# An attention block in fp32: how the second group's tokens are turned, and three places in VectorE's order

## The chip, the cores and the metric

The kernel runs on one core of a Trainium2 chip. A core has TensorE (matrix products, results into PSUM), VectorE, ScalarE and GpSimd (elementwise work), SyncE (which here only issues DMAs) and 16 DMA engines between the chip's memory (DRAM) and SBUF. Each engine works through its own list of instructions in order; a semaphore makes an instruction wait for another engine or for a DMA's landing. The metric is the device time of one execution in microseconds (us), lower is better. In the profile PE is TensorE, PEld its weight loads, DVE VectorE, ACT ScalarE, POOL GpSimd and SP SyncE; a `q` after a name (SPq) marks the engine's sequencer, which issues DMAs.

## The reference

The input `x` is 64 batches of 128 tokens with 512 features, all fp32. The reference normalises each token, takes 16 heads of queries (64 wide) and one head of keys and values that all heads share, puts a learned null key and value in front, adds an attention bias for each head, masks later tokens and masked tokens, and takes the softmax. The heads' results go through an output matrix, are normalised once more and are added to `x`:

```
xn = layernorm(x, g_in)
q = (xn @ Wq).reshape(b, n, H, DH).transpose(0, 2, 1, 3) * scale
k, v = split(xn @ Wkv);  null key and value in front
sim = einsum('bhid,bjd->bhij', q, k) + bias;  causal and token mask
out = einsum('bhij,bjd->bhid', softmax(sim), v) @ Wo
x = x + layernorm(out, g_out)
```

## The kernel before

The batches are worked on in groups of four (`GB = 4`; group g holds batches 4g to 4g+3) and in pairs. For each group the normalised tokens must stand with features on partitions (`xT[g]`), since TensorE multiplies along partitions. There are two ways to get there. `norm_T` (line 306 on) has TensorE transpose a batch's four 128x128 blocks against an identity into PSUM, and ScalarE copies them out in three pieces. `tokens_T` (line 321 on) has VectorE transpose 32x32 blocks in SBUF into a tile `xb`; when four such tiles are there, `tokens_out` stores `xb` to a DRAM buffer `xd` and `tokens_in` reads it back in four loads, in the order wanted. Before the change groups 0 and 1 go by `norm_T`, groups 2 to 15 by the other way. The two ways need different tiles from DRAM: for `norm_T` a tile is one batch (128 rows of `x[m]`, line 120), for `tokens_T` it is 32 tokens of each of the group's four batches (line 122). `xs[m]` is that tile for place m; place 4 lives in `wM`.

Everything stands in the order in which the program writes it (a manual schedule): the list at the file's end (from line 1559 on) for groups 0 and 1, then `body_first`, then `turn(d)` and `body(d)` for the pairs, `turn_end` and `body_end` for the last two pairs, and `body_last`. No planner moves anything.

In the first part stand, in this order on their engines: statistics of the tiles (`norm_stats`: three small VectorE operations and a power on GpSimd, line 281), the keys' and values' product (`kv_pair`, `kv_pair_out`: VectorE writes `vT` at line 380, ScalarE `kT` at line 390), the causal mask on the bias (`causal`, GpSimd, line 212), the subtraction of the null bias (`null_shift`, VectorE, line 229), mask and bias together (`bias_add`, GpSimd, line 683), scores on TensorE (line 718) and their addition to the bias on VectorE (lines 733 and 735), the exponentials on ScalarE (line 749). The queries of group 0 are full products (`q_mm`, line 450, copied out at line 459), those of later groups seven products of halves (`product`, line 515), in which product 7 adds into a PSUM tile after ScalarE has kept what was there (`keep`, line 527, tile `ku`). For these, VectorE makes sums of weights (line 483) and GpSimd sums of tokens (`token_sum`, line 497).

DMAs are nearly all issued by SyncE, in order, and each carries one of eight semaphores in turn: a DMA is issued only when the DMA eight places ahead of it has landed. In `body_end` the output products add into one PSUM tile (`py_s`) in turn; VectorE copies an intermediate result out (`out_keep` of `yu2`, line 948, tile `kyu`) and TensorE's next product into that tile waits for the copy.

## Time and profile before

| | us |
|---|---|
| median of 3 runs | 1023.34 (1023.27 to 1023.65) |
| profiled execution | 1022.89 |
| its span, first to last instruction | 1021.0 |
| TensorE busy in the span | 1013.0 (99%) |
| VectorE busy | 845.7 (83%) |
| GpSimd busy | 768.6 (75%) |
| ScalarE busy | 673.2 (66%) |

The profiled execution is 1.9 us longer than its span, which counts from the first to the last instruction. A row of the timeline gives start, duration, engine, line, operation, tiles written and read, and how many instructions it merges; in brackets stands how long the engine was idle before it and what ended that. TensorE's clock was granted at 0.998 of full speed.

### The profile page before, as it was taken

The page shows a single profiled execution, that of the slowest core. Times are in us where ns is not written, and L with a number is a line of the kernel's source. Part 1 is how long each engine was busy: PE and PEld are TensorE (multiplying, and loading weights), DVE is VectorE, ACT ScalarE, POOL GpSimd, SP SyncE. Part 2 cuts the span into 40 slices and gives each one's busy share as a digit, 9 for nine tenths or more (in the row PEclk, how much of TensorE's full clock was granted, in tenths as well). Part 3 has the DMA queues.
Part 4 walks back from the last instruction along what each step waited for, and adds up shares of the span by engine and source line. Part 5 has one row for each costly group of instructions (what it writes and reads, how often), then busy time and mean ns, then how long its engine had stood idle before and what let it go on. Part 6 is the DMA issues. An engine that isn't in the chain of part 4 may idle for free.

```text
span 1021.0 us, 31459 instructions
## 1 busy us (share of the span) xinstructions
PE 1013.0 (99%) x12333; PEld 901.6 (88%) x12333; DVE 845.7 (83%) x1958; ACT 673.2 (66%) x2753; POOL 768.6 (75%) x633
## 2 busy tenths in 40 slices
PE   9999999999999999999999999999999999999997
PEld 9888888888888888888888888888988888888886
DVE  6777888888888888888888888888898888977787
ACT  5766677656677665686656776566775657865583
POOL 4997768677686877859678696776868768686686
PEclk9999999999999999999999999999999999999999
DMA  7415243151431415225152340514314152140221
GB/s 218 139 30 150 67 125 111 34 154 63 145 97 69 123 56 152 87 75 140 35 152 85 109 123 29 164 63 138 103 49 134 64 153 89 70 113 24 69 85 62
DMA packets 73835, 100.86 MB, mean 99 GB/s; under 512 B 32212, under 2 KB 36056, under 8 KB 71896
## 3 DMA queue, kind: packets, MB, share of 16 engines
q1 hardware_dynamic: 73392, 98.47, 32.3%
q8 instruction: 96, 1.57, 0.6%
q14 instruction: 51, 0.42, 0.1%
q10 hardware_dynamic: 296, 0.40, 0.1%
HBM read 63.19 MB, written 33.55 MB: 95 GB/s over the span
## 4 chain that ended last, share of the span: by engine, by line
PE 97%; POOL 1%; DVE 1%; issue 0%; ACT 0%; POOLq 0%; DVEq 0%
PE pyX L936 20%; PE pa L515 16%; PE pyY L936 10%; PE pc L515 10%; PE po L849 8%; PE pkv L363 6%; PE pyw L936 5%; PE pl L581 4%; PE pm L647 4%; PE ps L718 3%; PE pq L450 3%; PE sc_X L718 2%; PE sc_Y L718 2%; PE sc_a L718 1%; PE py_s L936 1%; PE busy L1556 1%
## 5 line engine op out<-in xcount | busy, mean ns | idle before, releaser
L749 ACT ACTIVATE s<-s,nmax 128x65 f32<-128x65 f32 (+1 forms) x1024 | 372.1, 369 | 61.7 <-DVE nmax L740 61.7
L771 POOL TENSOR_TENSOR s<-s,rinv 128x512 f32<-128x512 f32 (+1 forms) x132 | 190.6, 1446 | 132.7 <-DVE rinv L767 132.7
L683 POOL TENSOR_TENSOR s<-biasp,mneg 128x1552 f32<-128x1552 f32 (+1 forms) x65 | 206.3, 3177 | 51.0 <-DVE s L733 27.0
L749 ACT ACTIVATION_READ_ACCUMULATOR s<-s,nmax 128x1 f32 x1024 | 197.0, 192 | 0.0
L787 DVE STREAM_TRANSPOSE sb<-s 128x1536 f32<-128x1536 f32 (+1 forms) x68 | 113.6, 1674 | 11.3 <-POOL s L771 11.3
L740 DVE TENSOR_REDUCE nmax<-s 128x8 f32<-128x1032 f32 (+1 forms) x128 | 121.7, 951 | 0.1
L964 ACT COPY y<-pyX 128x256 f32<-128x256 f32 x29 | 10.8, 372 | 167.5 <-PE pyX L936 161.2
L936 PE MATMUL pyX<-wT,oT 128*128 128x256 f32 x464 | 109.8, 380 | 0.0
L936 PE MATMUL pyX<-wo,oT 128*128 128x256 f32 x464 | 109.7, 380 | 0.0
L936 PEld LDWEIGHTS pyX<-wo,oT 128*128 128x128 f32 x464 | 86.2, 191 | 10.4
L936 PEld LDWEIGHTS pyX<-wT,oT 128*128 128x128 f32 x464 | 84.2, 191 | 9.1
L916 POOL TENSOR_TENSOR oT<-oT 128x512 f32<-128x512 f32 x64 | 80.5, 1277 | 3.9 <-PE pyw L936 1.6
L527 ACT COPY ku<-pa 128x256 f32<-128x256 f32 x118 | 43.4, 367 | 59.7 <-issue 30.8
L849 PE MATMUL po<-sb,vr 32*64 32x128 f32 (+1 forms) x3904 | 81.8, 308 | 0.0
L849 PEld LDWEIGHTS po<-sb,vr 32*64 32x64 f32 x3904 | 71.4, 131 | 8.3 <-issue 5.9
L536 DVE TENSOR_TENSOR qT<-pc,ku 128x256 f32<-128x256 f32 x118 | 48.1, 408 | 32.2 <-PE pc L515 19.9
L868 ACT ACTIVATE oT<-po,nv 128x512 f32<-128x512 f32 (+1 forms) x127 | 73.5, 655 | 0.5 <-PE po L849 0.4
L515 PE MATMUL pa<-xS,wq 128*128 128x256 f32 x264 | 67.8, 380 | 0.0
L597 DVE TENSOR_TENSOR qT<-pl,kp 128x128 f32<-128x128 f32 x112 | 32.0, 286 | 42.8 <-PE pl L581 41.9
L281 POOL TENSOR_TENSOR rstd<-rstd,nhalf 128x1 f32<-128x1 f32 x64 | 35.2, 558 | 42.2 <-DVE rstd L280 39.3
L363 PE MATMUL pkv<-xT,wkv 128*128 128x256 f32 x256 | 63.4, 391 | 0.0
L515 PE MATMUL pa<-xT,wq 128*128 128x256 f32 x236 | 60.6, 380 | 0.0
(207 smaller groups left out, 2591.9 us busy)
## 6 DMA issues: line engine op xcount, KB each, us to landing
res<-in_x_dram SPq DMA_DIRECT2D x64, 256.0 KB
out_dram<-y SPq DMA_DIRECT2D x63, 256.0 KB
x<-in_x_dram SPq DMA_DIRECT2D x62, 256.0 KB
xd<-xb SPq DMA_DIRECT2D x14, 1024.0 KB
xT<-xd SPq DMA_DIRECT2D x56, 256.0 KB
vr<-vd SPq DMA_DIRECT2D x64, 128.0 KB
kT<-kT SPq DMA_DIRECT2D x32, 64.0 KB
vd<-vb SPq DMA_DIRECT2D x32, 64.0 KB
```

The source lines that it names most:

```text
L363: nc.tensor.matmul(pkv, wkv[:, kc, :], xT[g][:, t : t + 2, kc, :], start=(kc == 0), stop=(kc == KC - 1),)
L515: nc.tensor.matmul(prod[tag], w[:, kc, f * P : (f + 1) * P], t[:, :, kc, :], start=(start and kc == 0), stop=(kc == HK - 1), skip_group_ch ...
L683: nc.gpsimd.tensor_tensor(S[b][:, :, keys], biasp[:, :, keys], mneg[:, t, keys] .unsqueeze(1) .broadcast_to([P, R8, keys.stop - keys.start ...
L718: nc.tensor.matmul(home[r][u * DH : (u + 1) * DH, f, :], qT[g, f, t // 2][rows, t % 2, hf, u], kT[rows, 0 : nk // Q, t, :], start=True, st ...
L740: nc.vector.tensor_reduce(nmax[b][:, hf], S[b][:, :, WITH_NULL[hf]], AX.X, ALU.max, negate=True)
L749: nc.scalar.activation(row, row, AF.Exp, bias=nmax[b][:, hf, k : k + 1], accum_out=rsum[b][:, hf, k : k + 1],)
L771: nc.gpsimd.tensor_tensor(sv, sv, rinvs[b, hf][:, lo:hi].unsqueeze(2).broadcast_to([P, hi - lo, sv.shape[2]]), ALU.mult,)
L787: nc.vector.transpose(sbs[b][:, :, lo:hi].rearrange("p j e q -> p e j q"), S[b][:, lo:hi, 1 : ROW - 1].rearrange("p e (j k) -> p e j k", k=Q),
L849: nc.tensor.matmul(po[s][rows, to : to + n], vr[g][quad, t, PLACE[j], :], sb[quad, slots, r * NF : (r + 1) * NF, :], start=(turn == 0), st ...
L868: nc.scalar.activation(to, src, AF.Identity, bias=nv2)
L916: eng.tensor_tensor(o, a, b, op)
L936: nc.tensor.matmul(prod[key], h[:, c, :], w[:, c, :], start=(start and c == 0), stop=(c == HC - 1), skip_group_check=not start,)
```

## The change

Group 1 goes by `tokens_T`, `tokens_out` and `tokens_in` instead of `norm_T`, so its four tiles are loaded by line 122. Three query products (columns 0, 1 and 2 for the group's second half of batches) now stand ahead of the second batch's scores, where there were two, and the first two of them are done in two halves of tokens each. `token_sum(1, 1)` and `(1, 2)` are written later, which leaves GpSimd's order as it was. In `body_end` a maximum over scores (`scores_max(b, 1)`) moves behind the copy `kyu`; in `body_last` the last statistics of one tile move ahead of the sum for the other.

```diff
-        if g < 2:
+        if g == 0:
             queue.dma_start(out=xs[m], in_=x[m])
         else:
             nc.sync.dma_start(
                 out=xs[m], in_=x[g * GB : (g + 1) * GB, t * Q : (t + 1) * Q, :]
...
-    def q_batches(cs):
+    def q_batches(cs, h=0):
...
         scale(b, 0)
-        scores_max(b, 1)
         out_product(p, 6, ps_s, "s", start=False)
         out_keep("s", "yu2", "yu2")
+        scores_max(b, 1)
...
         nc.vector.bn_stats(st[0][:, 1], ys[p][:, hi_e])
+        mv, rstd = last_stats(p, st[0])
         out_product(p, 7, ps_q, "c", start=False)
         out_part(p + 1, 1, "c", "yp5")
-        mv, rstd = last_stats(p, st[0])
...
-    norm_T(4)
+    tokens_T(4)
...
-    norm_T(5)
+    tokens_T(5)
     mask_neg(0)
     q_batches((6,))
-    norm_T(6)
+    tokens_T(6)
+    tokens_T(7)
+    tokens_out(1)
+    tokens_in(1)
     null_shift(0)
     bias_add(0, (slice(0, UK.start), slice(UK.start, ROW)))
     q_half(7, 0)
-    norm_T(7)
...
+    q_batches((0,), 1)
     exps(0, 0, 0, 4)
-    q_half(0, 1)
+    q_batches((1,), 1)
     exps(0, 0, 4)
-    q_half(1, 1)
+    q_half(2, 1)
```

On SyncE, in the first 20 us: `x_202`, `x_204`, `x_206` and `wM` are the tiles of places 5, 6, 7 and 4, `nkv` the null key and value, `biasp` the bias.

```order
 L174 DMA wkv<-in_L_cond_Wkv_dram 128x4x128
 L175 DMA wq<-in_L_cond_Wq_dram 128x4x512
-L120 DMA wM<-in_x_dram 128x512
-L120 DMA x_202<-in_x_dram 128x512
-L120 DMA x_204<-in_x_dram 128x512
-L120 DMA x_206<-in_x_dram 128x512
+L122 DMA wM<-in_x_dram 128x1x512
+L122 DMA x_202<-in_x_dram 128x1x512
+L122 DMA x_204<-in_x_dram 128x1x512
+L122 DMA x_206<-in_x_dram 128x1x512
 L180 DMA nkv<-in_cond_dram 128x1
 L198 DMA biasp<-in_fside_16xSxS_dram 64x4x64
```

The four loads keep their places and take the other form; further down SyncE's list, behind `vr` and ahead of `nv`, come the store to `xd` and the four loads of `xT`.

On VectorE, around the two subtractions of the null bias (line 229):

```order
 L289 TENSOR_SCALAR nmr_383<-mv_326,rstd_328 128x1
 L289 TENSOR_SCALAR nmr_385<-mv_340,rstd_342 128x1
+L326 STREAM_TRANSPOSE xb_399<-wM 128x4x4x32
 L225 COPY nbp<-nbh 64x8
 L229 TENSOR_TENSOR biasp<-biasp,nbp 64x8x192
+L326 STREAM_TRANSPOSE xb_399<-x_202 128x4x4x32
+L326 STREAM_TRANSPOSE xb_399<-x_204 128x4x4x32
+L326 STREAM_TRANSPOSE xb_399<-x_206 128x4x4x32
 L225 COPY nbp<-nbh 64x8
 L229 TENSOR_TENSOR biasp<-biasp,nbp 64x8x192
```

One transpose comes ahead of the first subtraction, three ahead of the second.

On VectorE in `body_end`, here for the pair before the last; first before the change, where `nmax` is the result of the maximum:

```order
L1142 TENSOR_SCALAR lrs_12982<-lmv_12980 128x1
L966 TENSOR_TENSOR y_13007<-pyw_2_13002,kyp_12989 128x256
L767 RECIPROCAL rinv_0_13011<-rsum_12991 128x8
L740 TENSOR_REDUCE nmax_12955<-s_12763 128x8
L948 COPY kyu_13020<-py_1_s 128x256
L767 RECIPROCAL rinv_1_13026<-rsum_12947 128x4
```

and after it:

```order
L1142 TENSOR_SCALAR lrs_12969<-lmv_12967 128x1
L966 TENSOR_TENSOR y_12994<-pyw_2_12989,kyp_12976 128x256
L767 RECIPROCAL rinv_0_12998<-rsum_12978 128x8
L948 COPY kyu_13006<-py_1_s 128x256
L740 TENSOR_REDUCE nmax_12942<-s_12750 128x8
L767 RECIPROCAL rinv_1_13013<-rsum_12934 128x4
```

Copy and maximum have changed places; nothing else in the pair has.

More of the change, by code (lines that the diff above doesn't have):

```diff
@@ L466, in q_half @@
         q_copy(pq, c, h)
-    def q_batches(cs):
-        pqs = [q_room(c, 0) for c in cs]
+    def q_batches(cs, h=0):
+        pqs = [q_room(c, h) for c in cs]
         for t in range(2):
             for pq, c in zip(pqs, cs):
-                q_mm(pq, c, 0, slice(t, t + 1))
+                q_mm(pq, c, h, slice(t, t + 1))
         for pq, c in zip(pqs, cs):
-            q_copy(pq, c, 0)
+            q_copy(pq, c, h)
     def weight_sum(k):
@@ L1631 @@
     bias_add(2)
+    q_batches((0,), 1)
     exps(0, 0, 0, 4)
-    q_half(0, 1)
+    q_batches((1,), 1)
     exps(0, 0, 4)
-    q_half(1, 1)
+    q_half(2, 1)
     rinv(0, 0)
     scale(0, 0)
-    token_sum(1, 1)
-    token_sum(1, 2)
     scores(1, 0, ((ps_y, "X"), (ps_w, "w")))
@@ L1645 @@
     scores_max(1, 1)
+    token_sum(1, 1)
+    token_sum(1, 2)
     exps(0, 1, 0, 4)
-    q_half(2, 1)
     exps(0, 1, 4)
```

## The prediction

> **What bounds the kernel now.** First the table of windows over one long stretch: its bounds and length, then busy time of TensorE, its weight loads, VectorE, ScalarE and GpSimd, clock, DMA share and GB/s.

> ```profile
> 10.00:960.00 950.00, 950.00 (x11464) 847.27 (x11463) 789.37 (x1832) 634.29 (x2590) 718.80 (x581) 1.00 0.34 99
> ```

> From 10 to 960 us TensorE has no idle time (950.00 of 950.00). Work taken from it there is a gain only if nothing else becomes late, and a stall put into the start is never won back: there is no later gap to swallow it. So I looked at who else runs close to the edge before 60 us. Timeline rows of VectorE, GpSimd, ScalarE and of TensorE's weight loads, start and duration first:

> ```profile
> 18.12 0.14 DVE L373 TENSOR_SCALAR nkv<-nkv 64x1 f32<-64x1 f32 x1
> ...
> 20.67 7.35 POOL L212 TENSOR_SCALAR_AFFINE_SELECT biasp<-biasp 64x512 f32<-64x512 f32 x6
> ...
> 23.56 1.75 DVE L229 TENSOR_TENSOR biasp<-biasp,nbp 64x1536 f32<-64x1536 f32 x1 [1.16 <-POOL biasp L212]
> ...
> 28.06 1.75 DVE L229 TENSOR_TENSOR biasp<-biasp,nbp 64x1536 f32<-64x1536 f32 x1 [2.21 <-POOL biasp L212]
> ...
> 29.96 9.73 POOL L683 TENSOR_TENSOR s<-biasp,mneg 128x520 f32<-128x520 f32 x4 [1.93 <-DVE biasp L229]
> ...
> 36.55 0.42 DVE L733 TENSOR_TENSOR s<-sc_w,s 128x256 f32<-128x256 f32 x1 [0.50 <-POOL s L683]
> ...
> 36.55:53.63 17.08, 17.08 (x81) 15.07 (x80) 16.73 (x24) 11.68 (x58) 17.00 (x11) 1.00 0.40 126
> ...
> 52.35 0.49 DVE L380 TENSOR_SCALAR vT<-pkv,nkv 64x256 f32<-64x256 f32 x1
> ...
> 52.92 0.76 ACT L390 ACTIVATE kT<-pkv,nkv 64x128 f32<-64x128 f32 x3 [2.27 <-DVE vT L380]
> ...
> 54.59 0.37 ACT L527 COPY ku<-pa 128x256 f32<-128x256 f32 x1 [0.20 <-PE pa L515]
> ...
> 55.04 0.84 PEld L515 LDWEIGHTS pa<-xS,wq 128*128 128x128 f32 x4
> ```

> Read from top to bottom this is one chain beside TensorE. GpSimd applies the causal mask (20.67 to 28.02), VectorE subtracts the null bias as soon as that ends (28.06), GpSimd adds mask and bias as soon as that ends (29.96), VectorE waits for the sums (36.55, 0.50 idle) and then works almost without a break until 53.63 (16.73 of 17.08). ScalarE waits 2.27 for its `vT`, writes `kT`, normalises a tile and copies `ku`; ScalarE could have copied `ku` 0.20 earlier, and TensorE loads the weights of product 7, which needs that copy, 0.08 after it ends (54.96 to 55.04). So the chain lies only 0.20 behind TensorE at 55 us: whatever delays line 373 at 18.12 or the mask at 20.67 by d delays TensorE there by d - 0.20.

> **The change part by part.** *Transposes taken from TensorE.*

> ```profile
> 22.36 0.60 PE L313 MATMUL pxT<-wR,wM 128*128 128x128 f32 x4
> 22.80 1.95 PE L450 MATMUL pq<-xT,wq 128*128 128x128 f32 x16
> 24.58 0.60 PE L313 MATMUL pxT<-wR,x 128*128 128x128 f32 x4
> ...
> 27.24 1.89 PE L450 MATMUL pq<-xT,wq 128*128 128x256 f32 x8
> 28.97 0.60 PE L313 MATMUL pxT<-wR,x 128*128 128x128 f32 x4
> ```

> One batch's four transposes hold TensorE for 0.44 (22.36 to 22.80), so four batches 1.76, and twelve ScalarE copies go with them. But the chain above doesn't use this: of the 1.76 only 0.20 could reach product 7. The two products cut into token halves take 1.78 instead of 1.73 each (22.80 to 24.58; 27.24 to 28.97): 0.1, inside that. Moving one more product ahead of the second scores adds nothing and moves ScalarE's copies little: nothing.

> *Transposes given to VectorE*: four operations like this one.

> ```profile
> 54.42 0.71 DVE L326 STREAM_TRANSPOSE xb<-x 128x512 f32<-128x512 f32 x1 [0.79 <-ACT x L302]
> ```

> The first (0.71) fits into the 1.16 idle before 23.56, the other three (2.13) into the 2.21 before 28.06. Nothing; without that cover 2.84.

> *The loads.* Batches 4 to 7 are now read as 4 batches x 32 tokens (line 122) instead of 128 rows of one batch (line 120). The trace has both. DMA share and GB/s are the last two figures of these windows; the first is in the stretch where line-120 and weight loads run, the others where only the two line-122 loads issued at 54.44 are under way:

> ```profile
> 11.50:12.50 1.00, 1.00 (x11) 1.00 (x11) 0.67 (x2) 0.37 (x1) 0.30 (x1) 1.00 1.07 397
> ...
> 57.50:58.50 1.00, 1.00 (x6) 0.90 (x5) 0.91 (x2) 0.42 (x2) 1.00 (x2) 1.00 0.26 102
> 60.50:61.50 1.00, 1.00 (x55) 0.91 (x57) 0.67 (x3) 0.00 (x0) 0.92 (x2) 1.00 0.27 100
> ...
> 54.44 1.14 SPq L122 DMA_DIRECT2D x<-in_x_dram  x2
> ```

> A line-122 load moves at 100 to 102 GB/s on a quarter of the DMA engines (share 0.26), and two of them issued together still hold only that quarter: they share the same four engines, one after the other. 256 KB takes 2.6 us there, against 0.67 at 397 GB/s. [...]

> ```profile
> SPq L184 <- DMA x<-in_x_dram: 0.7, 1, 0.7
> ...
> 13.78 0.69 DVE L270 BATCH_NORM_STATS2 st<-wM 128x6 f32<-128x512 f32 x1 [0.80 <-DMA wM<-in_x_dram]
> 16.35 0.57 SPq L184 DMA_DIRECT2D nbh<-cond_null_attn_bias_dram  x1
> 19.37 1.07 SPq L200 DMA_DIRECT2D biasp<-in_fside_16xSxS_dram  x2
> ...
> 28.17 1.17 SPq L189 DMA_DIRECT2D nv<-in_cond_dram  x2
> ```

> Batch 4 lands at 13.78 now (VectorE waits for it), so its data start near 13.11; at 2.6 each, batches 4 to 7 land at 15.7, 18.3, 20.9 and 23.5. Batch 7 landed by 16.35 before (that landing lets SyncE issue `nbh`): 7.15 later. Line 373 at 18.12 needs `nkv`, whose small load stands right behind batch 7; I take it 0.3 later, 23.8 (between 0 and the 0.57 of one issue). So VectorE's order, statistics of batches 5 and 6, `nkv`, `vT`, statistics of batch 7, then GpSimd's power and mask, moves by d = 23.8 - 18.12 = 5.7. The bias loads behind `nbh` move by 7.15: the last one, issued by 19.37 + 1.07 = 20.4, would be out by 27.6, and the second half of the mask wants it at 20.67 + 7.35/2 + 5.7 = 30.0: 2.4 us for a small load, just enough, no cost. Product 7 then comes 5.7 - 0.2 = **5.5** later, and with TensorE full up to 960 us so does everything behind it.

> *The round trip through DRAM*: one store and four loads, on SyncE ahead of `nv` and the next tiles.

> ```profile
> 80.03 0.33 SPq L335 DMA_DIRECT2D xd<-xb  x1
> 83.92 1.76 SPq L343 DMA_DIRECT2D xT<-xd  x4
> ...
> 84.30:91.60 7.30, 7.30 (x36) 6.43 (x35) 6.00 (x11) 1.48 (x6) 5.30 (x3) 1.00 0.90 201
> ...
> 40.63 2.28 POOL L497 TENSOR_TENSOR xS<-xT 128x512 f32<-128x512 f32 x1
> ```

> The store takes SyncE's slot of 28.17, 5.7 to 7.15 later: 33.9 to 35.3. The loads go 3.89 after it and their 1.05 MB are in between 5.6 us (at 201 GB/s) and 7.7 us (91.60) later: 43.4 to 46.9. GpSimd's first token sum wants them at 40.63 + 5.7 = 46.3. I take nothing; at the late end 0.6. The next tiles, `wo` and `gob` go out about 6 us later than the rest (3.89 to the loads' issue, 1.76 for it); their users are also later by 5.7, so nothing, with a microsecond of risk.

> *VectorE's order in the last steps.*

> ```profile
> 974.10 1.18 DVE L740 TENSOR_REDUCE nmax<-s 128x8 f32<-128x1032 f32 x1
> 975.19 0.42 DVE L948 COPY kyu<-py_s 128x256 f32<-128x256 f32 x1
> ...
> 975.75 1.97 PE L936 MATMUL py_s<-wo,oT 128*128 128x256 f32 x8 [0.28 <-DVE rinv L767]
> ...
> 994.37 1.97 PE L936 MATMUL py_s<-wo,oT 128*128 128x256 f32 x8 [0.38 <-DVE rinv L767]
> ...
> 999.07 1.91 DVE L787 STREAM_TRANSPOSE sb<-s 128x768 f32<-128x768 f32 x2
> ...
> 1001.04 0.45 PE L849 MATMUL po_s<-sb,vr 32*64 32x256 f32 x4
> ...
> 1012.82 1.27 POOL L1161 TENSOR_TENSOR y<-y,res 128x512 f32<-128x512 f32 x1
> 1014.04 0.55 POOL L1308 TENSOR_TENSOR rstdo<-rstdo,nhalf 128x1 f32<-128x1 f32 x1
> 1015.63 0.43 DVE L1275 BATCH_NORM_STATS2 stl<-pyc 128x6 f32<-128x256 f32 x1
> ```

> With the copy `kyu` ahead of the 1.18 maximum, TensorE's waits of 0.28 and 0.38 go. Next late is VectorE's transpose: it ends at 1000.98 and the last batch's values start at 1001.04, so much of the 0.66 returns there. I take half, **-0.3** (bounds -0.7 and 0). In the very last step the power on GpSimd can't start before the residual ahead of it ends (1014.09), and VectorE's later statistics wait for TensorE: nothing (bounds -0.3 and 0).

> The sum: +5.5 - 0.3 = +5.2. Span 1021.0 + 5.2 = 1026.2; the profiled execution 1022.89 + 5.2 = 1028.1. It ran 0.45 under the median of the runs, 1023.34, so the median after is **1028.5**.

> **The rivals.** *The loads are no later than before* (they spread, or are early enough): then the transposes' gain is cut to 0.2 by `ku`, and with the end's 0.3 the median is 1022.8, no change. This decides if batch 7 lands by 17.8, 0.3 ahead of line 373 at 18.12, so with 1.4 us of delay at most. Against it: the 0.26 share. *The whole gain arrives*: 1.76 + 0.66 = 2.4, 1020.9, faster. It needs the loads early and the chain behind 36.55 shorter; nothing in the change shortens that. *The round trip comes late too*: GpSimd waits at the token sum, or VectorE for the next tiles, 1 to 3 us on top, 1030.5. For it: the token sum's slack ends at -0.6. *TensorE's other stalls*: ScalarE, in order, copies queries behind the mask load, which moves too; if that runs past the chain, up to 1 us more, inside the range.

> **How the numbers follow.** Slow loads holding the chain: 0.79, 1028.5. Its low end: the four engines free 1 us earlier than 13.11 (-1.0), `nkv` and a `vT` (0.3 and, by the row at 52.35, 0.5) not on the way to the mask (-0.8), all 0.7 at the end (-0.4), and the 0.45 between profiled run and median: 1025.8. Round trip late as well: 0.13, up to 1030.5 + 1 for ScalarE + 0.5 = 1032.0. Loads hidden: 0.05. Whole gain: 0.03. The range holds the first two, 0.92 less their tails. A measurement here tells 0.2%, 2 us, from no change: slower 0.92, same 0.05, faster 0.03.

> **What would show it.** Right: `wM` and three tiles landing about 2.6 apart, VectorE idle for x loads between 14 and 24; line 373 near 23.8, the mask near 26.4, line 683 near 35.7; line 326 four times before 34 without moving line 229; product 7's weights near 60.5; no 0.28 and 0.38 in the last steps. Wrong: the mask still near 20.7, or TensorE without idle time before 60 us.

## The result, and the profile after

The changed kernel takes 1036.84 us (median; 1035.96 to 1038.73) against 1023.48 for the kernel before on the same chip: 1.0133 times as long, 95% interval 1.0120 to 1.0145, so 13.4 us slower where 5.2 were forecast; 1036.84 lies above the forecast's upper bound of 1032.0. The profiled execution took 1036.95, its span 1035.2 (before: 1022.89 and 1021.0), TensorE's clock 0.994.

The window that was full before (950.00 of 950.00), in the profile after; columns as in the prediction:

```profile
10.00:960.00 950.00, 940.57 (x11392) 836.74 (x11391) 781.10 (x1812) 625.40 (x2546) 708.34 (x577) 0.99 0.34 100
```

TensorE is idle for 9.4 us of it, and a clock of 0.99 where it was 1.00 says that it also worked more slowly for a while. The timeline after, in the order of the prediction's chain (loads, mask, bias):

```profile
15.56 0.70 DVE L270 BATCH_NORM_STATS2 st<-wM 128x6 f32<-128x512 f32 x1 [2.51 <-DMA wM<-in_x_dram]
...
21.41 0.69 DVE L270 BATCH_NORM_STATS2 st<-x 128x6 f32<-128x512 f32 x1 [1.40 <-DMA x<-in_x_dram]
...
24.40 0.15 DVE L373 TENSOR_SCALAR nkv<-nkv 64x1 f32<-64x1 f32 x1 [1.89 <-DMA nkv<-in_cond_dram]
...
25.11 0.76 ACT L390 ACTIVATE kT<-pkv,nkv 64x128 f32<-64x128 f32 x3 [6.29 <-DVE vT L380]
...
26.18 7.20 PE L450 MATMUL pq<-xT,wq 128*128 128x128 f32 x40 [3.78 <-ACT qT L459]
...
26.97 7.35 POOL L212 TENSOR_SCALAR_AFFINE_SELECT biasp<-biasp 64x512 f32<-64x512 f32 x6
...
31.65 1.90 DVE L326 STREAM_TRANSPOSE xb<-x 128x512 f32<-128x512 f32 x3
...
33.90 1.12 ACT L670 ACTIVATE mneg<-m,neg 128x256 f32<-128x256 uint8 x2 [2.98 <-DMA m<-in_mask_BxS_bk_dram]
...
35.32 0.27 PE L718 MATMUL sc_Y<-kT,qT 64*64 64x64 f32 x1 [1.47 <-ACT qT L459]
...
36.34 1.20 POOL L683 TENSOR_TENSOR s<-biasp,mneg 128x520 f32<-128x520 f32 x1 [2.02 <-DVE biasp L229]
```

The first half is as forecast: tiles one after the other, line 373 at 24.40 (23.8 forecast), the mask at 26.97 (26.4), line 683 at 36.34 (35.7), so the chain is 6.4 late instead of 5.7. New are TensorE's own waits, 3.78 and 1.47, both for ScalarE's copies of queries: ScalarE works in order and stood at `kT` for 6.29 (its releaser `vT` stands behind line 373 on VectorE) and then at the mask tile `m` for 2.98.

From the round trip to product 7:

```profile
36.56 0.37 SPq L335 DMA_DIRECT2D xd<-xb  x1
...
42.60 1.74 SPq L343 DMA_DIRECT2D xT<-xd  x4
...
51.25 1.27 POOL L497 TENSOR_TENSOR xS<-xT 128x512 f32<-128x512 f32 x1 [4.20 <-DMA xT<-xd]
...
53.55 0.69 DVE L270 BATCH_NORM_STATS2 st<-x 128x6 f32<-128x512 f32 x1 [2.77 <-DMA x<-in_x_dram]
...
57.95 0.69 DVE L270 BATCH_NORM_STATS2 st<-x 128x6 f32<-128x512 f32 x1 [3.30 <-DMA x<-in_x_dram]
...
58.97 1.77 DVE L787 STREAM_TRANSPOSE sb<-s 128x1536 f32<-128x1536 f32 x1
...
63.04 0.49 DVE L380 TENSOR_SCALAR vT<-pkv,nkv 64x256 f32<-64x256 f32 x1
...
64.97 0.36 ACT L527 COPY ku<-pa 128x256 f32<-128x256 f32 x1
65.43 2.04 PE L515 MATMUL pa<-xS,wq 128*128 128x256 f32 x4 [4.16 <-ACT ku L527]
```

The store's landing lets the loads go: 36.56 to 42.60, 6.0 us against 3.89 in the later steps of the kernel before. The token sum then waits 4.20, and VectorE waits 2.77 and 3.30 for tiles 8 and 9, which SyncE issues behind these transfers. Tile 9 comes last: behind its statistics stand VectorE's transpose, `vT`, ScalarE's `kT` and `ku` (54.59 before, 64.97 now). Product 7 starts 10.2 late.

The clock, in windows of 3.41 us of the profile after (columns as above; the last three are clock, DMA share, GB/s):

```profile
22.96:26.37 3.41, 0.20 (x1) 0.20 (x2) 1.80 (x6) 1.01 (x4) 0.27 (x2) 1.00 0.26 56
26.37:29.78 3.41, 3.41 (x17) 3.41 (x17) 2.31 (x7) 2.54 (x6) 3.27 (x4) 0.50 0.47 115
...
60.51:63.92 3.41, 0.76 (x4) 0.33 (x2) 3.35 (x8) 0.31 (x2) 3.41 (x3) 1.00 0.20 76
63.92:67.33 3.41, 1.90 (x5) 1.57 (x6) 1.11 (x3) 2.40 (x7) 3.41 (x3) 0.50 0.18 31
67.33:70.75 3.42, 3.42 (x10) 2.70 (x9) 1.55 (x4) 0.74 (x2) 3.42 (x2) 0.50 0.26 86
70.75:74.16 3.41, 3.41 (x54) 2.79 (x55) 2.43 (x3) 1.76 (x4) 3.33 (x3) 1.00 0.17 60
```

After a stretch in which TensorE worked 0.76 of 3.41 us (60.51 to 63.92), its clock is exactly half for two stretches: 5.32 us of work from 65.43 to 70.75 at half speed lose 2.66. The same happened once before, behind the wait of 3.78: 0.20 of 3.41 worked, then a whole stretch at half clock, which loses 1.7. That loss is part of how late TensorE itself comes to product 7 (it is ready for it at 61.27, 6.0 later than product 7 started before), so it isn't to be added to the 10.2. The first maximum over scores behind it comes 12.84 later than before (62.69 to 75.53): 10.2 and 2.6. Up to 147 us about 0.6 more is lost in small steps, the last pair's statistics (line 1275) come at 1029.18 against 1015.63, 13.55 later, and the last 0.65 of the 14.2 by which the span grew lie in the landing of the last stores. For these last two small amounts the traces show no cause.

### The profile page after: what moved, and what is told of

It is laid out like the page before. It is cut to its first block, busy times and chain, and to the rows that moved or that the text cites. A ratio compares the mean times of both kernels' runs of the same rounds, so it can differ in the third digit from the quotient of the medians.

```text
span 1035.2 us, 31459 instructions
## 1 busy us (share of the span) xinstructions
PE 1017.2 (98%) x12333; PEld 902.8 (87%) x12333; DVE 846.6 (82%) x1962; ACT 671.2 (65%) x2741; POOL 766.4 (74%) x633
## 4 chain that ended last, share of the span: by engine, by line
PE 92%; DMA 3%; DVE 1%; ACT 1%; POOL 1%; issue 1%; SPq 0%; POOLq 0%; DVEq 0%; ACTq 0%
PE pyX L936 19%; PE pa L515 15%; PE pyY L936 10%; PE pc L515 10%; PE po L849 8%; PE pkv L363 5%; PE pyw L936 5%; PE pl L581 4%; PE pm L647 4%; PE ps L718 3%; PE sc_X L718 2%; PE sc_Y L718 2%; DMA x<-in_x_dram 1%; DMA nkv<-in_cond_dram 1%; PE sc_a L718 1%; PE py_s L936 1%
## 5 line engine op out<-in xcount | busy, mean ns | idle before, releaser
L683 POOL TENSOR_TENSOR s<-biasp,mneg 128x1552 f32<-128x1552 f32 (+1 forms) x65 | 206.2, 3175 | 51.0 <-DVE s L733 25.0
L787 DVE STREAM_TRANSPOSE sb<-s 128x1536 f32<-128x1536 f32 (+1 forms) x68 | 113.6, 1675 | 11.5 <-POOL s L771 11.5
L740 DVE TENSOR_REDUCE nmax<-s 128x8 f32<-128x1032 f32 (+1 forms) x128 | 121.9, 952 | 0.1
L936 PE MATMUL pyX<-wT,oT 128*128 128x256 f32 x464 | 109.7, 379 | 0.0
L936 PE MATMUL pyX<-wo,oT 128*128 128x256 f32 x464 | 109.7, 379 | 0.0
L936 PEld LDWEIGHTS pyX<-wo,oT 128*128 128x128 f32 x464 | 86.0, 190 | 10.5
L936 PEld LDWEIGHTS pyX<-wT,oT 128*128 128x128 f32 x464 | 84.0, 190 | 9.2
L849 PE MATMUL po<-sb,vr 32*64 32x128 f32 (+1 forms) x3904 | 83.3, 308 | 0.2 <-DVE sb L787 0.2
L527 ACT COPY ku<-pa 128x256 f32<-128x256 f32 x118 | 43.4, 368 | 60.9 <-issue 30.9
L849 PEld LDWEIGHTS po<-sb,vr 32*64 32x64 f32 x3904 | 71.8, 130 | 9.6 <-issue 5.8
L515 PE MATMUL pa<-xS,wq 128*128 128x256 f32 x264 | 69.7, 387 | 4.2 <-ACT ku L527 4.2
L515 PEld LDWEIGHTS pa<-xS,wq 128*128 128x128 f32 x264 | 50.9, 194 | 11.7 <-issue 4.5
## 6 DMA issues: line engine op xcount, KB each, us to landing
xd<-xb SPq DMA_DIRECT2D x15, 1024.0 KB
```

The source lines that it names most:

```text
L515: nc.tensor.matmul(prod[tag], w[:, kc, f * P : (f + 1) * P], t[:, :, kc, :], start=(start and kc == 0), stop=(kc == HK - 1), skip_group_ch ...
L683: nc.gpsimd.tensor_tensor(S[b][:, :, keys], biasp[:, :, keys], mneg[:, t, keys] .unsqueeze(1) .broadcast_to([P, R8, keys.stop - keys.start ...
L740: nc.vector.tensor_reduce(nmax[b][:, hf], S[b][:, :, WITH_NULL[hf]], AX.X, ALU.max, negate=True)
L787: nc.vector.transpose(sbs[b][:, :, lo:hi].rearrange("p j e q -> p e j q"), S[b][:, lo:hi, 1 : ROW - 1].rearrange("p e (j k) -> p e j k", k=Q),
L849: nc.tensor.matmul(po[s][rows, to : to + n], vr[g][quad, t, PLACE[j], :], sb[quad, slots, r * NF : (r + 1) * NF, :], start=(turn == 0), st ...
L936: nc.tensor.matmul(prod[key], h[:, c, :], w[:, c, :], start=(start and c == 0), stop=(c == HC - 1), skip_group_check=not start,)
```

## The experiments

Times are medians, with the ratio to the kernel before on the same chip and its 95% interval. In kernels 1, 2, 7, 9 and 10 the loads of batches 4 to 7 have the other kernel's form, so that their tiles hold the tokens in an order that the rest of the kernel doesn't expect: every operation stays and the time can be read, but the output of these batches isn't the reference's.

| kernel | median, us | ratio |
|---|---|---|
| 1 before + loads by line 122 | 1030.19 | 1.0066 (1.0052 to 1.0080) |
| 2 after + loads by line 120 | 1029.16 | 1.0056 (1.0042 to 1.0069) |
| 3 after, tiles 8 and 9 split | 1031.55 | 1.0074 (1.0058 to 1.0089) |
| 4 before + the two moves at the end | 1023.01 | 0.9995 (0.9987 to 1.0004) |
| 5 after, tiles 4 to 9 split | 1029.20 | 1.0056 (1.0041 to 1.0071) |
| 6 after, wait filled | 1036.24 | 1.0132 (1.0115 to 1.0149) |
| 7 kernel 2, store first | 1023.71 | 1.0002 (0.9993 to 1.0012) |
| 8 kernel 5, store first | 1029.18 | 1.0058 (1.0041 to 1.0075) |
| 9 kernel 2 again | 1029.16 | 1.0055 (1.0043 to 1.0068) |
| 10 kernel 2, wait filled | 1029.76 | 1.0058 (1.0045 to 1.0070) |
| 11 after, store first | 1031.53 | 1.0080 (1.0064 to 1.0095) |

**1. The loads alone.** In the kernel before:

```diff
-        if g < 2:
+        if g == 0:
             queue.dma_start(out=xs[m], in_=x[m])
```

> The kernel before, with only the loads of batches 4 to 7 in the form of line 122 (its tiles then hold the tokens of these batches in another order, so the output of batches 4 to 7 is not the reference's; every operation stays). Theory A, the slow loads carry about half of the loss and the late round trip and next tiles the rest: the mask moves from 20.67 to near 27.0, product 7's weights from 55.04 to about 61.3 (+6.2), the median to 1029.7, and up to 2.6 more if TensorE's wait is long enough for its clock to drop, 1032.3 at most. Rival B, the loads are harmless and the loss is made by the round trip and the next tiles: below 1026. Rival C, the loads make the whole loss: 1035 or more.

Measured: 1030.19, +6.6. Rows of its timeline:

```profile
47.06 2.28 POOL L497 TENSOR_TENSOR xS<-xT 128x512 f32<-128x512 f32 x1
...
53.63 0.68 DVE L270 BATCH_NORM_STATS2 st<-x 128x6 f32<-128x512 f32 x1
...
61.83 1.03 PE L515 MATMUL pa<-xS,wq 128*128 128x256 f32 x4
```

No wait at the token sum or tile 9, and none at product 7 either: it comes 6.6 late because TensorE itself is that late by now. It had waited 3.57 and 1.00 for ScalarE, as in the changed kernel, and behind the first of these waits its clock was half for one stretch, 26.87 to 30.28 (busy for all of it, 1.7 lost). Theory A holds: the slow loads make half of the loss, and the chain and TensorE's own waits reach product 7 about equally late. The half clock that it allowed for came too, but at another place than it meant.

**2. The transposes and the round trip alone.** In the changed kernel:

```diff
-        if g == 0:
+        if g < 2:
             queue.dma_start(out=xs[m], in_=x[m])
```

> The changed kernel, with the loads of batches 4 to 7 in the form of line 120 as before (the transposed tiles then hold tokens in another order, so the output of batches 4 to 7 is not the reference's; every operation stays). Theory A: the store is issued near 28.2, its landing takes 3.9 to 6.0, the four loads 7.7 to 8.4 more, so they are in between 39.8 and 42.6 against 40.63 where the token sum wants them; the next tiles come at 44 to 49 against 46.2 and 47.2: together 0 to 2 us, 1023 to 1026, and no half clock. Rival B, the round trip and the next tiles are the larger part also without the slow loads: 1028 or more, with token sum and statistics waiting 3 us and more. Rival D, with the loads back the taken transposes pay: below 1022.5.

Measured: 1029.16, +5.6, and in kernel 9 the same again. Theory A's 0 to 2 us is refuted; rival B holds.

```profile
29.48 0.37 SPq L335 DMA_DIRECT2D xd<-xb  x1
...
35.62 1.74 SPq L343 DMA_DIRECT2D xT<-xd  x4
...
43.75 2.29 POOL L497 TENSOR_TENSOR xS<-xT 128x512 f32<-128x512 f32 x1 [2.45 <-DMA xT<-xd]
...
50.10 0.69 DVE L270 BATCH_NORM_STATS2 st<-x 128x6 f32<-128x512 f32 x1 [2.98 <-DMA x<-in_x_dram]
...
57.58 1.72 PE L515 MATMUL pa<-xS,wq 128*128 128x256 f32 x4 [3.36 <-ACT ku L527]
```

The round trip is late by itself: the store takes 6.1 (29.48 to 35.62), the token sum waits 2.45 and tile 9 is awaited for 2.98. The gain of the taken transposes only makes TensorE wait longer for `ku`. Product 7 starts 2.3 late in this profile (kernel 9: 3.2), and the stretch from 57.92 to 61.33 behind the wait ran at half clock, which loses another 1.7; theory A had said that there would be none.

**3. Tiles 8 and 9 in pieces of 32 rows.** In the changed kernel's `load_x`, for these two tiles:

```diff
-            nc.sync.dma_start(
-                out=xs[m], in_=x[g * GB : (g + 1) * GB, t * Q : (t + 1) * Q, :]
-            )
+            for i in range(GB):
+                nc.sync.dma_start(
+                    out=xs[m][i * Q : (i + 1) * Q],
+                    in_=x[g * GB + i, t * Q : (t + 1) * Q, :],
+                )
```

> The changed kernel, with batch tiles 8 and 9 each loaded by four transfers of 32 rows instead of one of 4 x 32 rows. Theory A, the last 3.2 us of the stall are tile 9, slow because it goes through four of 16 DMA engines beside the 2 MB of wo: both tiles land by 54, VectorE's transpose at 58.97 then waits only for GpSimd's scale that ends at 55.73, vT comes near 60, product 7 near 62.3; TensorE waits 1 us there, its clock stays 1.00, and the median is 1036.8 - 3.1 - 2.6 = 1031.1. Rival E, the queue's order and not the four engines makes the tiles late: they land within 1 us of 57.93 and the time stays between 1035.5 and 1038. Rival F, the token sum binds at the same place: product 7 moves by less than 1 us.

Measured: 1031.55, 5.3 less than the changed kernel, as theory A said. Its line numbers are 7 higher (277 for 270, 794 for 787, 522 for 515):

```profile
54.55 0.69 DVE L277 BATCH_NORM_STATS2 st<-x 128x6 f32<-128x512 f32 x1
...
56.48 1.78 DVE L794 STREAM_TRANSPOSE sb<-s 128x1536 f32<-128x1536 f32 x1 [0.83 <-POOL s L778]
...
63.23 1.10 PE L522 MATMUL pa<-xS,wq 128*128 128x256 f32 x4
```

Tile 9 no longer keeps VectorE waiting; what ends its idle time now is GpSimd's scaling, which stands behind the token sum in GpSimd's order. Product 7 is 2.2 earlier and runs at full speed. So tile 9 was the last to come, and next to it in lateness the token sum.

**4. The moves at the end alone.** In the kernel before:

```diff
-        scores_max(b, 1)
         out_product(p, 6, ps_s, "s", start=False)
         out_keep("s", "yu2", "yu2")
+        scores_max(b, 1)
...
+        mv, rstd = last_stats(p, st[0])
         out_product(p, 7, ps_q, "c", start=False)
         out_part(p + 1, 1, "c", "yp5")
-        mv, rstd = last_stats(p, st[0])
```

> The kernel before, with only the two moves of VectorE's operations in the last steps. Theory A: TensorE's waits of 0.28 and 0.38 near 975 and 994 go, and the last batch's values, which wait for VectorE's transpose near 1001, give it back: between 0 and -0.3, 1023.2 to 1023.5. Rival G, as predicted half of the 0.66 stays: 1023.2 or lower, with product 4 of the last pair starting 0.3 earlier than 1013.60. Rival H, later statistics delay the power on GpSimd at the very end: 1023.8 or more.

Measured: 1023.01 against 1023.56, an interval that holds no change.

```profile
1000.79 0.42 PE L849 MATMUL po<-sb,vr 32*64 32x256 f32 x1 [0.19 <-DVE sb L787]
...
1013.35 1.99 PE L936 MATMUL pyc<-wT,oT 128*128 128x256 f32 x8 [0.57 <-DVE y L966]
```

The waits of 0.28 and 0.38 are gone, a new one of 0.19 for VectorE's transpose stands where the prediction put it, and the last product starts 0.25 earlier (1013.60 before). In the time this can't be told from nothing: rival H (1023.8 or more) is refuted, theory A and rival G, which lie within 0.3 us of each other, can't be told apart by it.

**5. Tiles 4 to 9 in pieces of 32 rows.** The edit of 3 for all six tiles.

> The changed kernel, with batch tiles 4 to 9 each loaded by four transfers of 32 rows. Theory A: these go through 16 engines, but SyncE now issues 12 more transfers ahead of nkv, so batch 7 lands near 18.3 instead of 24.1 and the mask starts near 22.7; the token sum still waits 2 to 3 us for the round trip, product 7 starts near 58.1, TensorE's wait is under 3.4 us so that its clock stays 1.00: 1026.4, between 1025.5 and 1027.5. Rival: the transfers are bound by something other than the number of engines (the rows' addresses in DRAM, the number of issues); batch 7 lands after 22 and the time is 1029 or more.

Measured: 1029.20; the forecast of 1026.4 was wrong, though tile 7 had landed when VectorE came to it at 21.71 (25.10 in the changed kernel). Its timeline (line 219 for 212, 677 for 670, 725 for 718):

```profile
27.85 3.44 POOL L219 TENSOR_SCALAR_AFFINE_SELECT biasp<-biasp 64x512 f32<-64x512 f32 x3 [1.14 <-DMA biasp<-in_fside_16xSxS_dram]
...
31.61 1.12 ACT L677 ACTIVATE mneg<-m,neg 128x256 f32<-128x256 uint8 x2 [4.49 <-DMA m<-in_mask_BxS_bk_dram]
...
33.03 0.27 PE L725 MATMUL sc_Y<-kT,qT 64*64 64x64 f32 x1 [2.73 <-ACT qT L466]
```

Two of its clock stretches:

```profile
31.25:34.66 3.41, 1.63 (x47) 1.39 (x48) 1.93 (x3) 1.65 (x4) 1.39 (x3) 1.00 0.55 128
34.66:38.07 3.41, 3.41 (x17) 3.41 (x17) 2.66 (x5) 0.00 (x0) 3.41 (x2) 0.50 0.97 356
```

Twelve more transfers now stand ahead of the bias and the mask tile on SyncE, and each waits for the one eight places ahead: the 16 of tiles 4 to 7 hold SyncE from 6.00 to 18.91, 6.1 of it in waits, so about 0.4 goes to the issue of one. GpSimd waits for the bias, ScalarE 4.49 for the mask tile, and TensorE 2.73 for the queries that ScalarE copies behind it. The loads were cured (tiles 5 and 6 are read at 18.18 and 19.29, with no wait; 18.91 and 21.41 in the changed kernel) and the queue took their place. Theory A's full clock failed too: TensorE worked 1.63 of 3.41 us around its wait, and the next stretch ran at half, 1.7 us lost. The bound of 3.4 us on the wait was the author's estimate, and no run shows it: the wait here was 2.73, and in kernel 2 the half clock had come behind one of 3.36. The rival's time (1029 or more) was met, but not for its reason, since tile 7 was read before 22.

**6. TensorE's wait filled.** In the changed kernel, `body_first`, between products 6 and 7:

```diff
+        for _ in range(2):
+            for f in range(2):
+                product(g, f, 5, *rooms_c[f])
         norm_apply(m + 1)
```

> The changed kernel, with product 5 of both halves computed twice more between product 6 and product 7 (3.45 us of extra matmuls with the same result, inside TensorE's wait of 4.16). Theory A, the long wait itself drops TensorE's clock to half: with the wait filled to under 1 us product 7 still starts near 65.4, but its groups of four matmuls take 1.03 instead of 1.91 to 2.04 and the median falls by 2.6 to 1034.2. Rival, the slow matmuls after the wait have another cause (their data or PSUM rooms come late one by one): the time stays within 0.6 of 1036.8. Rival, the clock is dropped by the work done and not by the wait: slower than 1037.5.

Measured: 1036.24, and 2.6 had been expected: not confirmed. In the profiled execution tile 9 came at 59.20, 1.25 later than in the profile after, and 2.53 of wait were left:

```profile
64.04:67.45 3.41, 0.88 (x5) 0.72 (x5) 2.17 (x5) 2.59 (x7) 3.41 (x3) 1.00 0.13 22
67.45:70.86 3.41, 3.41 (x10) 2.66 (x9) 1.14 (x3) 0.86 (x3) 3.41 (x2) 0.50 0.22 70
```

The wait fell into one stretch, with 0.88 of 3.41 busy, and the half clock followed. So a wait of 2.53, shorter than a stretch, was enough here. The time lies within 0.6 of 1036.8, where the rival (another cause of the slow matmuls) put it, so this run doesn't refute the rival; experiment 10 asks again.

**7. The store ahead of vr.** In kernel 2, the four loads of `vr` for group 0 (which the values product needs only near 63 us) are taken out of `values_T` into a function of their own, and called behind the store:

```diff
     tokens_out(1)
+    values_in(0)
     tokens_in(1)
```

> The kernel of the second experiment (loads in the form of line 120; the output of batches 4 to 7 is not the reference's), with the store of the transposed tokens issued ahead of the four loads of vr, and these between the store and its loads. Theory A, the 5.6 us lost there come from the queue: the store stood behind vr on SyncE and on the DMA engines. It is issued near 27.9 instead of 29.48, lands by 32.3 instead of 35.60, xT is in by 40 instead of 43.53, the token sum waits for nothing, tile 9 lands near 46.5 instead of 50.08 and waits at most 0.5; no half clock: 1023.0 to 1024.0. Rival, the round trip is slow by itself (store and loads take as long wherever they stand): 1027 or more. Rival, VectorE's four transposes cost what they take: 1025 to 1026.

Measured: 1023.71, ratio 1.0002: the 5.6 are gone, theory A holds. (Line 504 for 497, 534 for 527, 522 for 515.)

```profile
27.14 0.36 SPq L335 DMA_DIRECT2D xd<-xb  x1
...
32.01 2.32 SPq L343 DMA_DIRECT2D xT<-xd  x4
...
40.57 2.28 POOL L504 TENSOR_TENSOR xS<-xT 128x512 f32<-128x512 f32 x1
...
54.22 0.36 ACT L534 COPY ku<-pa 128x256 f32<-128x256 f32 x1
...
54.68 1.10 PE L522 MATMUL pa<-xS,wq 128*128 128x256 f32 x4 [1.07 <-issue]
```

The store lands after 4.9, the token sum waits for nothing, and TensorE, with 1.76 us of transposes less, waits 1.07 ahead of product 7. The profile names no releaser there; that it is the old chain is read from `ku`, which ends at 54.58. So VectorE's transposes and the round trip can be had for nothing where the loads are those of line 120, and the transposes taken from TensorE then bring next to nothing, as the prediction's first step says.

**8. Both repairs.** The edits of 5 and 7 together, in the changed kernel.

> The changed kernel with both repairs: tiles 4 to 9 by four transfers of 32 rows each, and the store ahead of the loads of vr. Theory A: only the later landing of batches 4 to 7 is left, about 2 us against before, less the 0.2 by which TensorE was behind: 1025.0, between 1024 and 1026; the token sum waits for nothing. Rival, the two repairs hinder each other in SyncE's queue: 1026.5 or more.

Measured: 1029.18, as kernel 5; expected 1025.0. That is the rival's time (1026.5 or more), but that the two repairs hinder each other isn't shown: once the tiles are split, moving the store changes nothing in the time. The queries behind the mask tile keep TensorE 3.09 (kernel 5: 2.73), the stretch from 33.65 to 37.06 behind that wait runs at half clock as in kernel 5, and at product 7 TensorE waits for nothing: it is late by itself.

**9 and 10. The wait filled, with the fast loads.** Kernel 9 is kernel 2 again; kernel 10 adds the edit of 6 to it.

> The kernel of the second experiment once more (loads in the form of line 120; the output of batches 4 to 7 is not the reference's), for a comparison on one chip with the next one: 1029.2, 1027.7 to 1031.6 as before, with one stretch of 3.41 us at half clock from product 7 on.

> The same kernel with product 5 of both halves computed twice more (3.45 us, same result) in TensorE's wait of 3.36 ahead of product 7. Theory A, the clock is granted by stretches of 3.41 us according to TensorE's busy share in the stretch before (half clock after 0.48 and less, full after 0.57 and more, in the traces so far): with the wait filled no stretch is under a half, product 7's groups of four take 1.03, and the median is 1.7 (half of 3.41) below the kernel without the filling. Rival: the slow groups after the wait are late data: the medians differ by less than 0.5. Rival: the filling delays product 7 by more than the clock gives back: slower than without.

Measured: 1029.16 and 1029.76, no gain in the time. The windows, laid on each execution's own clock stretches, of kernel 9 and then of kernel 10:

```profile
52.00:55.41 3.41, 1.81 (x9) 1.25 (x7) 3.41 (x6) 0.00 (x0) 3.25 (x4) 1.00 0.26 100
55.41:58.82 3.41, 0.36 (x2) 0.37 (x3) 2.55 (x5) 2.19 (x7) 3.41 (x2) 1.00 0.04 12
58.82:62.23 3.41, 3.41 (x10) 2.69 (x9) 0.45 (x2) 1.22 (x3) 3.41 (x3) 0.50 0.32 70
```

```profile
54.94:58.36 3.42, 2.43 (x12) 1.80 (x10) 2.81 (x4) 1.25 (x4) 3.42 (x3) 1.00 0.12 44
58.36:61.77 3.41, 2.84 (x13) 2.55 (x14) 1.57 (x4) 2.20 (x6) 3.41 (x2) 1.00 0.25 42
```

What concerns the clock came as forecast. Behind the stretch with 0.36 busy the next one ran at half, behind that with 2.43 at full speed, and the first groups of product 7 took 1.03 to 1.10 instead of 1.31 to 1.91. In kernel 10 tile 9 and with it product 7 came 0.47 later (58.93 against 58.46), and yet the maximum over scores behind it is 1.21 earlier (66.40 against 67.61): 1.68 won, half of 3.41. But at 947 us kernel 10 is 0.48 behind. TensorE has five waits ahead of `pkv` products there, and the profile gives them to no releaser:

```profile
PE pkv L363 <- issue: 1.3, 5, 0.4
```

They add up to 1.3 of the 1.7 lost again. Why these come up with the filling, and not in kernel 9, stays open; neither rival says it (product 7 came 0.47 later, less than the 1.68 that the clock gave back). So the half clock is shown to follow the idle stretch and to cost 1.7 where it stands; that taking it away shortens the whole kernel is not.

**11. The changed kernel with the store ahead of vr.** The edit of 7 in the changed kernel.

> The changed kernel, loads as changed, with only the store of the transposed tokens moved ahead of the loads of vr. Theory A: what is left is the slow loads alone, as in the first experiment: the mask near 27.0, no wait of 2.5 or more for the token sum or tiles 8 and 9, product 7 near 61.5, TensorE waiting less than 0.5 there; 1030.2, between 1029 and 1031.5. Rival: with the loads late the round trip stays late whatever the queue's order, 1034 or more.

Measured: 1031.53, 5.3 less than the changed kernel and at the upper edge of theory A, 1.3 above kernel 1. Rows (lines 270 and 522 for 515):

```profile
55.23 0.69 DVE L270 BATCH_NORM_STATS2 st<-x 128x6 f32<-128x512 f32 x1
...
62.71 1.10 PE L522 MATMUL pa<-xS,wq 128*128 128x256 f32 x4 [1.53 <-issue]
```

With the loads as late as in the changed kernel, moving one store on one queue takes away the wait for tile 9 and for the token sum. Product 7 is at 62.71 instead of 65.43. Theory A had it near 61.5 with a wait under 0.5; TensorE waits 1.53 there, for which the profile names no releaser, and it ran at half clock for two stretches, 24.93 to 31.76. The rival (1034 or more) is refuted.

No kernel here is faster than the one before by more than a measurement tells.

## Why the prediction was wrong, by its own steps

*What bounds the kernel* (TensorE full, a chain 0.20 behind it, nothing later to win a stall back): right. The delay behind product 7 is still there at 978 us: the maximum over scores of 964.94 before comes at 978.39, 13.45 later (12.84 at 75 us).

*Transposes taken from TensorE* ("of the 1.76 only 0.20 could reach product 7"): right in kind. In kernel 7, in which nothing else is late, product 7 starts at 54.68 against 55.25, 0.57 earlier where 0.20 were forecast, after a wait of 1.07 and with no gain that can be told in the time.

*Transposes given to VectorE* ("nothing"): right; line 326 ran four times between 27.87 and 33.55, and kernel 7 costs nothing.

*The loads* (+5.5): right in mechanism, a little small. The chain was 6.4 late instead of 5.7, and kernel 1 gives +6.6 for the loads alone. The prediction saw the delay only along VectorE and GpSimd. It named ScalarE's copies behind the mask load as a rival worth up to 1 us; in fact ScalarE, held by `kT` and the mask tile, made TensorE wait 3.78 and 1.47 and cost it a stretch at half clock (1.7), which brings TensorE itself to product 7 about as late as the chain.

*The round trip* ("I take nothing; at the late end 0.6", the next tiles "nothing, with a microsecond of risk"): this is the step that failed. It measured 4.0 at product 7 (10.2 less 6.2, which is the chain's 6.4 without the 0.20; 3.6 by the 6.6 of kernel 1), and 5.6 in the time of kernel 2, without the slow loads, in whose profile one stretch ran at half clock (1.7). Each of its terms was too small. The store was issued at 36.56, where 33.9 to 35.3 were forecast. It was priced by its 3.89 in the later steps, where nothing is moving ahead of it (a DMA share of 0.00 from 76 to 80 us); here it stands behind the four loads of `vr` and took 6.0. Ahead of them it took 4.9 (kernel 7) and 4.3 (kernel 11), so `vr` explains 1.1 to 1.7 of the 2.1, and the rest stays open. The four loads took 8.6 from first issue to the token sum's start, where 5.6 to 7.7 were counted (1.05 MB at 201 GB/s are 5.2; the 5.6 come out with the 0.4 from the loads' issue to the start of that window). And the next tiles, priced at nothing because their users "are also later by 5.7", stand behind all of this on SyncE: their issue is 16.3 later than before (29.39 to 45.66), tile 9 lands 18.3 later (39.64 to 57.93), and its reader wanted it 7.5 later (47.19 to 54.65). The rival "the round trip comes late too" named both waits; its 0.13 was too little, and its 1 to 3 us too small.

*Missing altogether*: the clock. No term held that TensorE runs slower after a wait, as it did here. That is 2.6 us behind product 7 in the profiled execution, and 1.7 more at 26.37 to 29.78, inside TensorE's own lateness.

*The end* (-0.3, bounds -0.7 and 0): right in its working and too small to be told. The new wait of 0.19 for VectorE's transpose is in the changed kernel too, at 1014.45.

Together, against the profiled execution before: +10.2 and +2.6 at 75 us, +0.6 by 147, nothing at the end, 0.65 behind the last statistics: 14.1 of the 14.2 are located, against 5.2 forecast. For 12.8 of them the cause is told above, for 1.3 it isn't known. The two parts do not simply add: 6.6 and 5.6 give 12.2, the change 13.4.

## What to carry to other kernels

A step that is moved to DMA must be priced in its place in the queue: what the same transfer takes later in the kernel, with a free queue, was a third too little here (3.89 for 6.0), and what was issued behind it went out late (the next tiles 16.3). Before taking work from the engine that is full, look for the chain that runs just behind it; here it let through 0.6 of 1.76 us at most, and with the new delays the kernel became 13.4 us slower. Where a wait left the matrix engine busy for 0.48 of a clock stretch or less, the next stretch ran at half clock in these traces (with one exception, at 0.42 in the window in which kernel 6's last product ends), 1.7 us where it stands; that this lengthens the whole kernel wasn't shown (kernel 10).

## What the runs showed of the hardware

*A line-122 load, with other loads queued behind it.* Two of them in the profile before move at a DMA share of 0.26, and the traces of the kernels before and after record the landing of a line-122 load in 4 parts and that of a line-120 load in 16: tile 4 lands in 16 parts from 12.62 to 13.76 before, in 4 from 15.13 to 15.54 after. Each of the four loads of `vr`, into 32 partitions, lands in 16 (the first from 36.70 to 37.04 after). Tiles 8 and 9 land 4.4 apart in the profile after (53.53 and 57.93), and before (35.26 and 39.64, with `wo` issued behind them at 31.22); the two loads issued at 54.44 before land 2.6 apart (60.14 and 62.80), where little else is moving (92 GB/s from 57.50 to 62.50). In the profile after, the 2 MB of `wo`, issued from 49.39 on behind tile 9 and a mask tile, move at the same time: the DMA engines' share from 53.55 to 57.95 is 1.06, at 258 GB/s. That `wo` is the cause is argued, since no run moved it. Split into pieces of 32 rows both tiles were in when VectorE came to them, at 53.49 and 54.55 (kernel 3, where `wo` was issued only at 52.83). That the pieces' own issues then make what stands behind them late is what kernel 5 shows (its first bias load was issued at 19.41, at 14.60 in the changed kernel).
